# A mixture-of-experts kernel: one more product split by a second Strassen–Winograd level, other places for the W2 mixtures, and another order in the last part

## The chip, the cores and the metric

The kernel runs on one core of a Trainium2 chip. The metric is device time in microseconds (us) for one launch. All arithmetic of the stages told of here is in fp32.

## The reference, cut to what matters

Eight sequences of 1024 tokens with 512 features go through two sublayers. The first is a causal attention whose queries, keys and outputs are built from table sines and cosines; the change does not touch it. The second is a feed-forward with eight experts:

```python
x = x + attention(layernorm(x))
x = x + ffn(layernorm(x))

probs = softmax(x @ Wr + br);  topk_p, topk_e = top_k(probs, 2)
# each of the 8 sequences has 160 places at each expert; later tokens are dropped
buf = zeros((8, 8 * 160, 512)).at[expert, sequence, place].add(x_rep * keep)
h = relu(einsum('enc,ech->enh', buf, W1) + b1)      # 512 -> 2048
y = einsum('enh,ehc->enc', h, W2) + b2              # 2048 -> 512
out[token] = sum over its two experts of y * probability * keep
```

So each of the eight experts multiplies 1280 rows by its W1 (512 x 2048) and its W2 (2048 x 512). This takes about three fifths of the kernel's time.

## The kernel before, in words

**Stages.** Attention runs over 32 pairs of a sequence and a group of four heads (scores at L683, exponentials at L703, values at L717), the router's steps lie beside it. Then come the experts, in 16 *parts*: for each expert one part of three pairs of row blocks (`nh` = 3, even number i) and one of two (`nh` = 2, odd i). A row block is 128 rows; a pair of them makes the upper and the lower half of a matrix product. Part 0 is the first, part 15 the last.

**Both layers by Strassen–Winograd.** Each product of two matrices is cut into 2 x 2 blocks and done with seven products, p1 to p7, of mixtures (sums and differences) of the blocks instead of eight plain ones. `gather(i)` fetches a part's rows by indirect DMA on POOL, transposes them on PE and forms the mixtures of the rows. `mix_w1(i, q)` forms the mixtures of W1 for one of eight column groups q, `mix_w2(e)` those of W2: four subtractions on DVE (L1067 to L1070) for each of eight slices k, one `yield` a slice, so that the caller can place them between other work. `load_w2` brings W2 in by eight DMAs of 512 KB.

**Layer 1.** For each q, a `Hidden` object runs p1 to p7 (L1239) and leaves the seven mixtures of the hidden values in `hid`. The p7 and p4 of one q are issued within the next (`layer1(this, before, final)`). After each product a `Hidden` takes one step of each generator in its `asides`.

**Layer 2, part 0.** `layer2(i, block, hid, aside)` does one pair of blocks with seven products of eight matmuls of 128 x 256 (one per slice k; each fp32 matmul shows as two instructions in the profile), L1340. Three such calls make up part 0's second layer.

**Layer 2, parts 1 to 15.** `layer2_quad` does two pairs of blocks at once. Four of the products are plain (L1473); the pair (part of `hid`, weight) names them: 0·0, 4·3, 5·4 and 6·5. The other three, 1·1, 2·2 and 3·6, are split once more by the same scheme: `SECOND` lists them, `mix` (L1422 to L1429) forms eight mixtures of their operands on DVE, and `second_level` runs seven chains of 128 x 128 matmuls (L1439) into three PSUM banks, with ACT copies (L1450 to L1464) and three DVE additions. `places` finds room for these mixtures: with `nh` = 2 in columns of `hid` that are not in use, with `nh` = 3 in new tiles of the gather's pools. Parts with `nh` = 3 do their third pair of blocks by `layer2` after the quad. Below, "quad" is a call of `layer2_quad`, and "run" is one product by the second level.

**Outputs.** For each pair of blocks, y1 (upper rows) and y2 (lower rows) are built in SBUF in left and right halves (y11, y12, y21, y22). `gate` multiplies by the router's probability (ACT, L1310), `send` adds the rows to `out` by an indirect DMA on POOL (L1315). Two of these may hit the same rows of `out`, so each waits for the one before it. The y tiles come from the pool `yp` with four buffers.

**What sets the order.** PE, ACT, DVE and SP run their instructions in the order in which the program issues them; the program interleaves by hand, with the generators (`next` is one step, `some(n, g)` is n steps, `rest(g)` what is left). PSUM has a pool of six banks for products, `ps_p`. In the loop over the parts, W2's mixtures for an expert are issued one slice per q from q = 2 on, the remaining ones before the second layer; for part 0 two slices are issued after q = 6 and the others after layer 1, right ahead of its second layer. In a part with `nh` = 2 the generator `aside` (the gather of the next part) is issued in steps within the quad, with `nh` = 3 and in part 0 within `layer2`. The core of that loop:

```python
for q in range(NHQ):
    ...
    if i and q > 1:
        next(mixes, None)
    tiles = layer1(Hidden(i, q, parts, hid, [ending]), tiles, q == NHQ - 1)
    ...
    elif i == 0 and q == NHQ - 2:
        mixes = mix_w2(0)
        some(2, mixes)
if i == 0:
    find_rows(1)
rest(mixes)
```

Of the kernel before, what the change touches and what calls it, by code (L numbers as in the profile page):

```python
# [11 lines left out]
F32 = mybir.dt.float32  # L12
# [9 lines left out]
P = 128  # L22
# [51 lines left out]
def preln_attn_moe_kernel(  # L74
# [106 lines left out]
    ident = const.tile([P, P], F32, name="ident")  # L181
# [876 lines left out]
    def mix_w2(e):  # L1058

        w = w2_tiles[e]  # L1060
        t = pools["w2p"].tile([P, NHQ, 3, DC], F32, name="w2_t")
        b11, b12 = w[:, :, 0, :DC], w[:, :, 0, DC:]
        b21, b22 = w[:, :, 1, :DC], w[:, :, 1, DC:]
        t2, t3, t4 = (t[:, :, n, :] for n in range(3))
        w2_tiles[e] = [b11, b21, b22, b12, t2, t3, t4]
        for k in range(NHQ):
            TT(t3[:, k, :], b12[:, k, :], b22[:, k, :], ALU.subtract)  # L1067
            TT(b12[:, k, :], b12[:, k, :], b11[:, k, :], ALU.subtract)  # L1068
            TT(t2[:, k, :], b22[:, k, :], b12[:, k, :], ALU.subtract)
            TT(t4[:, k, :], b21[:, k, :], t2[:, k, :], ALU.subtract)  # L1070
            yield
# [231 lines left out]

    def outputs(i, block):
# [9 lines left out]
        def send(r, y):  # L1314
# [5 lines left out]
            if i == 0:  # L1320
                tc.keep_in_program_order(ins)

# [6 lines left out]
    def layer2(i, block, hid, aside):  # L1329
# [8 lines left out]
        def product(ps, part, weight, first, last):  # L1338
# [5 lines left out]
            next(aside, None)  # L1344

        gate, send = outputs(i, block)
        (y1, y11, y12), (y2, y21, y22) = new_y(), new_y()
        low, high = b2_tiles[e][:, :DC], b2_tiles[e][:, DC:]

        def side_product():  # L1350
            side = bank()
            product(side, 1, 1, True, True)
            TT(y11, y11, side, ALU.add)
# [4 lines left out]
        nc.scalar.copy(y11, top)  # L1358
        if plain_first:
            side_product()  # L1360
        mid = bank()
        product(mid, 4, 3, True, False)
        nc.scalar.copy(y22, mid)
        product(top, 5, 4, False, False)
        nc.scalar.copy(y12, top)
        if not plain_first:
            side_product()
            product(top, 6, 5, False, False)
            TT(y22, y22, top, ALU.add)
        product(mid, 2, 2, False, True)  # L1370
# [3 lines left out]
        send(0, y1)  # L1374
        if plain_first:
            product(top, 6, 5, False, False)
            TT(y22, y22, top, ALU.add)
        TT(y22, y22, high, ALU.add)
# [4 lines left out]
        send(1, y2)  # L1383

# [17 lines left out]
    SECOND = [(1, 1), (2, 2), (3, 6)]  # L1402

    def layer2_quad(i, hid, aside, before_last):

        e = chunks[i][0]
        ws = w2_tiles[e]
        free = places(i, hid)
        low, high = b2_tiles[e][:, :DC], b2_tiles[e][:, DC:]
        two = range(2)  # L1410

        def split(t, part_of):
            return [[part_of(t[:, 4 * k : 4 * k + 4], c) for c in two] for k in two]

        def mix(n):
            part, weight = SECOND[n]
            a = split(hid, lambda t, c: t[:, :, part, c * P : (c + 1) * P])
            b = split(ws[weight], lambda t, c: t[:, :, c * P : (c + 1) * P])
            (a11, a21), (a12, a22) = a
            (b11, b12), (b21, b22) = b  # L1420
            t1, t2, t3, t4, s2, s3, s4 = free[:7]
            TT(t1, b12, b11, ALU.subtract)  # L1422
            TT(s3, a11, a21, ALU.subtract)
            TT(a21, a21, a22, ALU.add)
            TT(t2, b22, t1, ALU.subtract)
            TT(s2, a21, a11, ALU.subtract)
            TT(t3, b22, b12, ALU.subtract)
            TT(s4, a12, s2, ALU.subtract)
            TT(t4, b21, t2, ALU.subtract)  # L1429
            return (  # L1430
                (a11, b11), (a12, b21), (s4, b22), (a22, t4), (a21, t1), (s2, t2), (s3, t3)
            )
# [4 lines left out]
        def chain(ps, pair, first):  # L1437
            for k in range(4):
                nc.tensor.matmul(  # L1439
                    ps, lhsT=pair[0][:, k, :], rhs=pair[1][:, k, :], start=first and k == 0,  # L1440
                    stop=k == 3, skip_group_check=True,
                )

        def second_level(n, pairs):
            m1, m2, m3, m4, m5, m6, m7 = pairs
            c = free[7 + n]
            c11, c12, c21, c22 = (c[:, k, :] for k in range(4))
            u, v, z = (bank()[:, :P] for _ in range(3))
            chain(u, m1, True)
            nc.scalar.copy(c11, u)  # L1450
            next(aside, None) if n < 2 else None
            chain(v, m5, True)
            nc.scalar.copy(c21, v)
            chain(u, m6, False)
            nc.scalar.copy(c12, u)
            chain(z, m2, True)
            TT(c11, c11, z, ALU.add)
            chain(u, m7, False)
            nc.scalar.copy(c22, u)
            chain(v, m3, False)  # L1460
            TT(c22, c22, c21, ALU.add)
            TT(c12, c12, v, ALU.add)
            chain(u, m4, False)
            nc.scalar.copy(c21, u)  # L1464
            return [c[:, 2 * b : 2 * b + 2, :] for b in two]

# [3 lines left out]
        def product(ps, part, weight, first, last):  # L1470
            for b in two:
                for k in range(NHQ):
# [6 lines left out]

        gate, send = zip(*(outputs(i, b) for b in two))  # L1480
        some(2, aside)
        pairs = mix(0)
        top, mid = bank(), bank()
# [366 lines left out]
```

## Time and profile before

| | us |
|---|---|
| median of three runs | 3196.95 (3196.12 to 3196.96) |
| the profiled execution | 3195.52 |
| its span, which the profile's times refer to | 3193.8 |
| TensorE clock granted, mean | 0.997 |

By stage, from the windows view of the trace (times from the span's start):

| stage | from – to | length | PE busy | DVE busy |
|---|---|---|---|---|
| attention, router, first gather | 0 – 1258 | 1258.0 | 1206.9 | 1004.1 |
| layer 1 of part 0, with the last router steps | 1258 – 1342 | 84.0 | 81.6 | 55.7 |
| second layer of part 0 | 1342 – 1422 | 80.0 | 77.0 | 28.4 |
| layer 1 of part 1 (two pairs of blocks) | 1422 – 1470 | 48.0 | 48.0 | 29.1 |
| quad of part 1 | 1470 – 1516.3 | 46.3 | 46.3 | 36.5 |
| layer 1 of part 2 (three pairs of blocks) | 1516.3 – 1588.5 | 72.2 | 72.2 | 46.3 |
| quad and third pair of part 2 | 1588.5 – 1659.1 | 70.6 | 70.6 | 40.1 |
| quad of part 15 | 3132.8 – 3179.3 | 46.5 | 46.4 | 25.8 |
| tail after the last matmul | 3179.3 – 3193.8 | 14.5 | 0 | 0.4 |

Parts 3 to 14 repeat parts 1 and 2. A busy PE is one that has a matmul under way; the ends of matmuls are modelled, so the distance between starts is the better measure of what one costs. Idle time in front of an instruction is given in brackets with what ended it. The profile's line numbers are those of the kernel before.

### The profile page before, as it was taken

The page shows a single profiled execution, that of the slowest core. Times are in us where ns is not written, and L with a number is a line of the kernel's source. Part 1 is how long each engine was busy: PE and PEld are TensorE (multiplying, and loading weights), DVE is VectorE, ACT ScalarE, POOL GpSimd, SP SyncE. Part 2 cuts the span into 40 slices and gives each one's busy share as a digit, 9 for nine tenths or more (in the row PEclk, how much of TensorE's full clock was granted, in tenths as well). Part 3 has the DMA queues.
Part 4 walks back from the last instruction along what each step waited for, and adds up shares of the span by engine and source line. Part 5 has one row for each costly group of instructions (what it writes and reads, how often), then busy time and mean ns, then how long its engine had stood idle before and what let it go on. Part 6 is the DMA issues. An engine that isn't in the chain of part 4 may idle for free.

```text
span 3193.8 us, 51293 instructions
## 1 busy us (share of the span) xinstructions
PE 3122.6 (98%) x19726; PEld 2145.4 (67%) x19726; DVE 2209.3 (69%) x4643; ACT 1664.9 (52%) x2554; POOL 426.8 (13%) x387
## 2 busy tenths in 40 slices
PE   5999999999999999999999999999999999999998
PEld 2444444444444444689698698698698698698687
DVE  8888878888788775637657657656657656656654
ACT  7888888888888885413423423323323323323322
POOL 3000202020111123411011011011011011011010
PEclk9999999999999999999999999999999999999999
DMA  5435454554645353423423433434433334334331
GB/s 166 147 100 165 120 159 132 148 140 138 184 108 159 80 166 88 141 60 98 147 57 98 140 62 103 130 63 112 120 70 110 115 74 114 107 80 116 96 60 21
DMA packets 288547, 358.72 MB, mean 112 GB/s; under 512 B 28376, under 2 KB 199088, under 8 KB 276272
## 3 DMA queue, kind: packets, MB, share of 16 engines
q1 hardware_dynamic: 264944, 312.20, 33.3%
q0 software_dynamic: 22912, 43.22, 7.4%
q8 instruction: 157, 2.57, 0.4%
q14 instruction: 86, 0.70, 0.1%
q10 hardware_dynamic: 448, 0.02, 0.0%
HBM read 207.02 MB, written 81.22 MB: 90 GB/s over the span
## 4 chain that ended last, share of the span: by engine, by line
PE 79%; DVE 3%; ACT 1%; issue 1%; DMA 0%; SPq 0%; POOLq 0%; DVEq 0%; ACTq 0%
PE ps_p L1239 30%; PE ps_p L1473 13%; PE av L717 9%; PE ps_p L1439 9%; PE ps_s L683 9%; PE ps_p L1340 7%; ACT e L703 1%; PE ps_s L215 1%; PE ps_s L697 1%; DVE qk_f L524 1%; DVE qk_r L447 0%; DVE xT L837 0%; DMA qk<-qk_r 0%; DVE v L447 0%; SPq L608 0%
## 5 line engine op out<-in xcount | busy, mean ns | idle before, releaser
L703 ACT ACTIVATE e<-ps_s 128x1024 f32<-128x1024 f32 (+1 forms) x640 | 569.6, 937 | 183.3 <-PE ps_s L683 110.2
L683 PE MATMUL ps_s<-qk 64*128 64x512 f32 (+3 forms) x3072 | 597.3, 505 | 28.6 <-DMA qk<-qk_r 12.4
L717 PE MATMUL av<-e,v 128*64 128x512 f32 (+3 forms) x3072 | 523.4, 490 | 0.0
L683 PEld LDWEIGHTS ps_s<-qk 64*128 64x128 f32 x3072 | 262.3, 187 | 216.1 <-issue 106.4
L717 PEld LDWEIGHTS av<-e,v 128*64 128x64 f32 x3072 | 200.5, 137 | 283.1 <-issue 267.1
L1239 PE MATMUL ps_p<-xe,w 128*128 128x256 f32 (+1 forms) x1024 | 317.6, 433 | 1.1 <-issue 1.1
L1239 PE MATMUL ps_p<-xe_s,t 128*128 128x256 f32 (+1 forms) x1024 | 317.7, 433 | 0.0
L1239 PE MATMUL ps_p<-xe,t 128*128 128x256 f32 (+1 forms) x1024 | 317.7, 433 | 0.0
L1315 POOL DMA_INDIRECT out_dram<-y,slots x80 | 127.1, 1589 | 1234.0 <-ACT y L1310 1016.6
L768 POOL DMA_INDIRECT slot_d<-token,slot x128 | 159.2, 1244 | 988.5 <-issue 612.3
L1282 DVE TENSOR_TENSOR hid<-hid 128x256 f32<-128x256 f32 (+1 forms) x128 | 64.0, 500 | 283.0 <-ACT hid L1280 283.0
L1239 PEld LDWEIGHTS ps_p<-xe_s,t 128*128 128x128 f32 x1024 | 193.8, 190 | 82.0 <-ACT hid L1249 2.5
L1239 PEld LDWEIGHTS ps_p<-xe,t 128*128 128x128 f32 x1024 | 194.2, 190 | 80.4 <-issue 0.4
L1239 PEld LDWEIGHTS ps_p<-xe,w 128*128 128x128 f32 x1024 | 193.7, 190 | 79.4 <-issue 1.2
L1473 PE MATMUL ps_p<-w_t,hid 128*128 128x256 f32 x960 | 212.2, 379 | 0.0
L1473 PE MATMUL ps_p<-w,hid 128*128 128x256 f32 x960 | 209.6, 379 | 0.0
L1473 PEld LDWEIGHTS ps_p<-w,hid 128*128 128x128 f32 x960 | 182.4, 190 | 26.3
L1473 PEld LDWEIGHTS ps_p<-w_t,hid 128*128 128x128 f32 x960 | 180.1, 190 | 23.2
L1239 PE MATMUL ps_p<-xe_s,w 128*128 128x256 f32 (+1 forms) x512 | 158.9, 433 | 0.6 <-ACT p L1255 0.6
L1249 ACT COPY hid<-ps_p 128x256 f32<-128x256 f32 (+1 forms) x128 | 54.2, 423 | 179.6 <-PE ps_p L1239 170.9
L1340 PE MATMUL ps_p<-w,hid 128*128 128x256 f32 x640 | 144.8, 381 | 2.5 <-DVE w L1068 2.5
L697 PEld LDWEIGHTS <-keys_b 64*128 64x128 bf16 x1536 | 80.8, 95 | 89.5 <-issue 71.5
(300 smaller groups left out, 4959.6 us busy)
## 6 DMA issues: line engine op xcount, KB each, us to landing
w<-in_L_ffn_W_dram SPq DMA_DIRECT2D x256, 256.0 KB, 3.4
w<-in_L_ffn_W_dram SPq DMA_DIRECT2D x64, 512.0 KB, 7.4
qk<-qk_c SPq DMA_DIRECT2D x124, 256.0 KB, 4.5
qk<-qk_r SPq DMA_DIRECT2D x120, 256.0 KB, 4.5
qk_base<-base_d SPq DMA_DIRECT2D x28, 1024.0 KB, 7.5
xn_d<-xn SPq DMA_DIRECT2D x72, 256.0 KB, 2.4
rows_d<-xg SPq DMA_DIRECT2D x70, 256.0 KB, 2.1
x_mid<-in_L_attn_x_dram SPq DMA_DIRECT2D x16, 1024.0 KB, 8.9
```

The costliest lines, as they stand in the source:

```text
L683: nc.tensor.matmul(ps[:, a, at : at + w], lhsT=pair[r, 1, kb * P : (kb + 1) * P], rhs=pair[r, 0, q0 : q0 + w], start=at == 0, stop=not own ...
L697: nc.tensor.matmul(out_, lhsT=keys_b[r, part, :], rhs=late, start=False, stop=part == 1, skip_group_check=True,)
L703: nc.scalar.activation(e, ps[:, :, :n], AF.Exp, scale=UNIT * UNIT / math.sqrt(2 * DH))
L717: nc.tensor.matmul(av[a * 64 : (a + 1) * 64, q0 - 512 * h :], lhsT=vt[:, kb, 2 * pr + a, :], rhs=es[i][:, a, at : at + w], start=kb == 0, ...
L768: queued = nc.gpsimd.indirect_dma_start(out=slot_d[b], out_offset=bass.IndirectOffsetOnAxis(ap=idx, axis=0), in_=src, in_offset=None,)
L1239: nc.tensor.matmul(ps, lhsT=weights[:, k, :], rhs=rows[:, k, :], start=first and k == 0, stop=last and k == 1, skip_group_check=True,)
L1249: nc.scalar.copy(self.blocks[0], self.top)
L1282: TT(g1, g3, h22, ALU.add)
L1315: ins = nc.gpsimd.indirect_dma_start(out=out, out_offset=bass.IndirectOffsetOnAxis(ap=meta[:, e, jj[r], 0:1], axis=0), in_=y, in_offset=No ...
L1340: nc.tensor.matmul(ps, lhsT=hid[:, k, part, cols], rhs=ws[weight][:, k, :], start=first and k == 0, stop=last and k == NHQ - 1, skip_group ...
L1439: nc.tensor.matmul(ps, lhsT=pair[0][:, k, :], rhs=pair[1][:, k, :], start=first and k == 0, stop=k == 3, skip_group_check=True,)
L1473: nc.tensor.matmul(ps[:, b * DC : (b + 1) * DC], lhsT=hid[:, k, part, b * P : (b + 1) * P], rhs=ws[weight][:, k, :], start=first and k == ...
```

## The change

**A fourth product by the second level.** In all 15 quads p5 (product 4·3) becomes a run too. A class `Second` replaces `SECOND`, `mix` and `second_level`: `weights()` and `left()` are generators of four DVE operations each for the two sides, `both()` issues them interleaved, `run()` issues the chains. In parts with `nh` = 2 the weights of p5 and p2 are mixed within layer 1 (two operations at each of q = 3 to 6), their left sides in the quad; in parts with `nh` = 3 both sides are mixed in the quad. The order of a quad becomes: plain 0·0, run of p5, plain 5·4, run of p2, plain 6·5, run of p3, [with `nh` = 3: two products of the third pair of blocks], run of p4. `layer2` is now a generator that yields after each product, so that the third pair can be issued in pieces.

**W2's mixtures in smaller portions.** `mix_w2` yields after each subtraction. In part 0 the mixtures are created after q = 4 and one operation is handed out per product in q = 6, two per product in q = 7; the rest follows layer 1, ahead of `find_rows(1)` (before, behind it). In the other parts four operations are issued at q = 2 and 3 and eight from q = 4 on.

**The last part.** Its order becomes: runs of p2, p3 and p4, then the plain product 6·5 by blocks, with y21 and y22 built beforehand. y1 is gated and sent within the run of p4. The four scatters of the last part wait for the last one of part 14 and are declared free of each other.

**Pools.** `ident` gets its place from another pool, and `yp` has five buffers instead of four.

The diff, cut:

```diff
@@ mix_w2
-            TT(t3[:, k, :], b12[:, k, :], b22[:, k, :], ALU.subtract)
-            ...
-            yield
+            for to, x1, x2 in ((t3, b12, b22), (b12, b12, b11), (t2, b22, b12), (t4, b21, t2)):
+                TT(to[:, k, :], x1[:, k, :], x2[:, k, :], ALU.subtract)
+                yield
@@ outputs: send
+            if i + 1 == len(chunks):
+                tc.add_manual_dep(ins.ins, sent[i - 1][-1].name, ...)
+                for other in sent.get(i, ()):
+                    tc.declare_no_dep(ins.ins, other, reason="rows of their own")
+            sent.setdefault(i, []).append(ins.ins)
@@
+    class Second:
+        OPERANDS = {2: (1, 1), 3: (2, 2), 4: (3, 6), 5: (4, 3)}
...
+        def weights(self):
+            ...
+            for to, x1, x2 in ((t3, b22, b12), (t1, b12, b11), (t2, b22, t1), (t4, b21, t2)):
+                TT(to, x1, x2, ALU.subtract)
+                yield
+        def left(self):
+            ...
+            for to, x1, x2, op in (
+                (s3, a11, a21, ALU.subtract), (a21, a21, a22, ALU.add),
+                (s2, a21, a11, ALU.subtract), (s4, a12, s2, ALU.subtract),
+            ):
+                TT(to, x1, x2, op)
+                yield
+        def both(self):
+            w, a = self.weights(), self.left()
+            for gen, count in ((w, 2), (a, 2), (w, 1), (a, 1), (w, 1), (a, 1)):
+                some(count, gen)
+            ...
+        def run(self, c, between=lambda: None, late=lambda: None):
+            ...
+            chain(u, a11, b11, True)
+            nc.scalar.copy(c11, u)
+            between()
+            chain(v, a21, t1, True)
+            nc.scalar.copy(c21, v)
+            chain(u, s2, t2, False)
+            nc.scalar.copy(c12, u)
+            chain(z, a12, b21, True)
+            TT(c11, c11, z, ALU.add)
+            chain(u, s3, t3, False)
+            nc.scalar.copy(c22, u)
+            late()
+            chain(v, s4, b22, False)
+            TT(c22, c22, c21, ALU.add)
+            TT(c12, c12, v, ALU.add)
+            chain(u, a22, t4, False)
+            nc.scalar.copy(c21, u)
@@ layer2_quad
+        last_part = nh == 2
+        ask(2)
+        if last_part:
+            rest(second[5].left())
+        else:
+            second[5].both()
         product(top, 0, 0, True, False)
         for b in two:
             nc.scalar.copy(y11[b], of(top, b))
-        product(mid, 4, 3, True, True)
-        some(3, aside)
-        c = second_level(0, pairs)
-        ...
+        if last_part:
+            rest(second[2].left())
+        ask(2)
+        five = second[5].run(c5)
+        second[3 if last_part else 2].both()
+        ask()
         product(top, 5, 4, False, False)
         for b in two:
             nc.scalar.copy(y12[b], of(top, b))
-            TT(y12[b], y12[b], of(mid, b), ALU.add)
+        add_to(y12, five)
+        add_to(y11, second[2].run(c, ask))
+        second[4 if last_part else 3].both()
+        ask()
+        if i + 1 == len(chunks):
+            add_to(y12, second[3].run(c))
+            ...
+            four = second[4].run(c, late=first_rows)
+            for b in two:
+                TT(as_pair(y21[b]), as_pair(low), four[b], ALU.add)
+                TT(as_pair(y22[b]), as_pair(high), five[b], ALU.add)
+            for b in two:
+                product(top, 6, 5, False, True, [b])
+                for y in (y22[b], y21[b]):
+                    TT(y, y, of(top, b), ALU.add)
+                    gate[b](1, y)
+                send[b](1, y2[b])
+            return extra
         product(top, 6, 5, False, True)
+        for b in two:
+            TT(as_pair(y22[b]), as_pair(of(top, b)), five[b], ALU.add)
...
+        add_to(y12, second[3].run(c, ask))
...
+        if not last_part:
+            first_rows()
+            second[4].both()
+            some(2, extra)
+        before_last()
...
+        add_to(y21, second[4].run(c5, right_halves, first_rows if last_part else lambda: None))
@@ the loop over the parts
+            if nh == 2:
+                second = seconds(i, hid)
+                early_sums = itertools.chain(second[0][5].weights(), second[0][2].weights())
...
-                    next(mixes, None)
+                    some(4 if q < 4 else 8, mixes)
+                if 2 < q < 7:
+                    some(2, early_sums)
+                beside = [ending] if i or q < NHQ - 2 else [mixes] * (q + 3 - NHQ)
-                tiles = layer1(Hidden(i, q, parts, hid, [ending]), tiles, q == NHQ - 1)
+                tiles = layer1(Hidden(i, q, parts, hid, beside), tiles, q == NHQ - 1)
                 if i == 0 and q == NHQ // 2:
...
-                elif i == 0 and q == NHQ - 2:
                     mixes = mix_w2(0)
-                    some(2, mixes)
+            rest(mixes)
             if i == 0:
                 find_rows(1)
-            rest(mixes)
```

## The prediction

> **What bounds the kernel now.** I read the page first: parts 1 and 2 (who is busy, and when), then the chain that ended last, and then the timeline of the stages that the diff touches.
>
> ```profile
> span 3193.8 us, 51293 instructions
> PE 3122.6 (98%) x19726; PEld 2145.4 (67%) x19726; DVE 2209.3 (69%) x4643; ACT 1664.9 (52%) x2554; POOL 426.8 (13%) x387
> ...
> PE ps_p L1239 30%; PE ps_p L1473 13%; PE av L717 9%; PE ps_p L1439 9%; PE ps_s L683 9%; PE ps_p L1340 7%; ACT e L703 1%; PE ps_s L215 1%; PE ps_s L697 1%; DVE qk_f L524 1%; DVE qk_r L447 0%; DVE xT L837 0%; DMA qk<-qk_r 0%; DVE v L447 0%; SPq L608 0%
> ```
>
> PE is busy for the whole span, and in the expert stages the chain hardly leaves it. There a microsecond of PE work is a microsecond of time, as long as DVE and ACT keep their work beside it. A busy share does not give the price of one matmul, though, so the timeline of PE is next, in the second layer of part 2:
>
> ```profile
> 1602.39 1.05 PE L1439 MATMUL ps_p<-w,hid 128*128 128x128 f32 x8
> 1603.28 1.06 PE L1439 MATMUL ps_p<-xe,hid 128*128 128x128 f32 x8
> ...
> 1608.64 7.07 PE L1473 MATMUL ps_p<-w_t,hid 128*128 128x256 f32 x32
> 1615.55 1.05 PE L1439 MATMUL ps_p<-w,hid 128*128 128x128 f32 x8
> ```
>
> Starts count here, not durations, which overlap. A plain product over two blocks (32 instructions, since each fp32 matmul is two) takes 1615.55 - 1608.64 = 6.91 us, or 215.9 ns each. A second-level product (7 chains of 8) takes 1608.64 - 1602.39 = 6.25 us, 0.893 us a chain, 111.6 ns each. No row between carries an idle time.
>
> Two places are not bound by PE's own work. In part 0's second layer PE waits for the W2 mixtures on DVE, and then runs slowly (columns of the second view: PE, PEld, DVE, ACT and POOL busy, PEclk, DMA share, GB/s):
>
> ```profile
> 1353.87 1.20 PE L1340 MATMUL ps_p<-w,hid 128*128 128x256 f32 x2 [1.01 <-DVE w L1068]
> 1355.59 1.22 PE L1340 MATMUL ps_p<-w,hid 128*128 128x256 f32 x2 [0.51 <-DVE w L1068]
> 1356.60 5.68 PE L1340 MATMUL ps_p<-w_t,hid 128*128 128x256 f32 x16
> ```
> ```profile
> 1357.00:1359.00 2.00, 2.00 (x6) 1.61 (x5) 0.00 (x0) 0.22 (x1) 0.00 (x0) 0.50 0.58 185
> ```
>
> At the very end PE has finished (3179.26 by the chain), and the last two scatters stand in a row:
>
> ```profile
> 3179.28 0.27 ACT L1464 COPY hid<-ps_p 128x128 f32<-128x128 f32 x1 [1.52 <-PE ps_p L1439]
> ```
> ```profile
> 3180.62 1.55 POOL L1315 DMA_INDIRECT out_dram<-y,slots  x1 [5.01 <-ACT y L1310]
> 3186.14 1.56 POOL L1315 DMA_INDIRECT out_dram<-y,slots  x1 [3.97 <-DMA out_dram<-y,slots]
> ```
>
> **What the skill says.** TensorE: Matmul & The Clock Gate, "Wait — 56ns, not 53.3ns?": warm matmuls start N / 2.4 GHz plus about 2.5 ns apart. The trace fits if an fp32 pass takes two cycles a column: 512 / 2.4 + 2.5 = 215.8 against 215.9 ns; 256 / 2.4 + 2.5 = 109.2 against 111.6 ns. The fixed part is why a split product saves less than one eighth. The same page, "What's actually happening": the clock is halved after about 3.4 us of idleness and comes back after about as much work. The trace agrees on 0.50, but here waits of at most 1.01 us each, close together, were enough. PSUM — Partial Sum Buffer, "PSUM bank collisions raise a hardware error": access has to be guarded by bank, not by address; the trace before has no such wait in the quad. DMA: Bandwidth & Descriptors, "Two DMAs through the same engine are not ordered": only a completion semaphore orders them; the 3.97 us above are such an order.
>
> **The change, part by part.** The first 1316 us have the same instructions in the same order on every engine (ident only changes its pool), so they stay.
>
> *p5 by the second level*, in all 15 quads (parts 1 to 15): one 6.91 us product out, one 6.25 us run in. -0.656 x 15 = **-9.8 us**, if nothing waits. DVE gets 8 mixing operations of 0.605 us (pitch) and 3 additions of 0.29 us, 5.7 us more a quad (its 16 y operations only change operands); ACT gets five copies of 0.27 us and loses two of 0.37. What hides them:
> - Three-block parts (7): p5's mixtures used to have p1 and p5 in front of them, 13.8 us; now p1 alone, 6.91. At 1588.57 the products began and the layer-1 tail left DVE at 1592.7, 4.1 us in. Then come t3, t1, s3, a21: a21 is done at about +6.6, and chain 2 wants it at 6.91 + 0.89 = +7.8. t2 and s2 come at 7.8 for +8.7, s4 at 9.0 for +11.4. Margin 0.9 to 1.2 us. It holds because W2's mixtures are no longer at this place: rows 1592.59 to 1596.02 of DVE held 3.4 us of them. They go to q 4 to 6 of layer 1, as four more operations (1.8 us) a round, where DVE idled 1.9 to 3.6 us before L1282. Almost full, not over.
> - Two-block parts (8): weight mixtures of p5 and p2 (two per round, 1.3 us) go into q 3 to 6, where the 64 rounds idle 127.6 / 64 = 2.0 us before L1282. The left sides need 4 operations, done at about +5.5 against +7.8.
> - Later runs: 8 mixtures end 5.6 us after the run before, and a 6.91 us step lies between (in three-block parts two products of the third block take that place before the last run).
> - The gather's transposes and sums (six and four) crowd DVE around p3's run: behind until about 17.6 us after p2's run, while layer 1 wants t1 at 20.7. ACT's first copy there is about 0.8 us early.
> - SP's order is unchanged. W2's next load may start later, when p3's run has read W2, but 6.25 us ahead of the quad's end; b2's load, in front of it, went out only 3.5 us ahead (1512.83, next part at 1516.3). POOL's order is the same too; y1's scatters wait longer, and the fifth y buffer covers that.
>
> *W2 mixtures of part 0 per product.* The stage should take 21 products of 3.453 us = 72.5 us and takes 1421.60 - 1341.82 = 79.8; lost 7.25 us. 0.65 of it is the wait for y at L1377, whose order stays. Now 21 of the 32 operations lie within layer 1 (8 before), in DVE's idle 3.9, 1.9 and 1.5 us there; 11 remain. By DVE's pitches of 0.34 to 0.46 us the last b12 is ready at about 1351.5, and PE wants it at 1348.73 + 7 x 0.432 = 1351.75. W2 is there: the eight loads land 1322 to 1333. The index row for part 1's gather now stands behind these 11, so its four gathers on POOL start 6.5 us later; its rows are due 50 us on. **-6.4 us** (-3 if PE waits once more and the clock falls; -6.6 at best).
>
> *Last part.* The final product comes by blocks, block 1 in block 0's bank. In the built program its first matmul waits for DVE's second read of that bank: two additions at 0.335 us pitch and a hop, about +0.95 us on PE. No row before shows it: 0 to 1.3. After PE's end two additions, two gates of 0.5 us and POOL: the last scatter starts at about +1.5, where it was 3186.14 - 3179.26 = +6.9. Block 0's has left 4 us earlier, and the y1 scatters earlier still. From there to the end 7.66 us as before. -5.4 + 0.95 = **-4.4 us** (-3 to -5.4).
>
> Sum: -9.8 - 6.4 - 4.4 = -20.6 us. The profiled execution took 3195.52 (span 3193.8 and 1.7 around it), so 3174.9; the median shown is 1.4 above that execution: **3176.3 us**.
>
> **The rivals.** Main case, 0.80: 3174 to 3179.
> *Only p5 pays*, 0.08: PE still waits in part 0, or the bank wait and slow gates eat the end: -9.8 and about 2 more, 3185. For it: both places hang on margins under 0.5 us. Against: two thirds of the mixtures do move.
> *Quads wait a little*, 0.07: 0.4 us each, from halved cover, x 15 = 6 us: 3182. For it: margins near 1 us, and a fuller DVE. Against: each is positive, from rows measured in the same stage.
> *Slower*, 0.05: a late a21 or t2 stops PE at chain 2 or 3 of the new run, in all quads; waits close together halve the clock, as in part 0, where 2.5 us of shown waits cost some 6.6. The point is 20.6 / 15 = 1.4 us a quad. DVE would have to be 2.5 us later than I place it, for instance if rounds with eight W2 operations no longer fit and leave it behind; then 2 us a quad with its clock make about 5: 15 x 5 - 20.6 = +54, 3251. Against: 1.8 us fits the idle time, and q 7 has no mixture any more.
> That the chains do not shorten PE can be left out: three such runs a quad are in the trace.
>
> **How the numbers follow.** 0.2% is 6.4 us, about what a measurement can tell. Main case, "only p5" and most of "waits a little" lie beyond it: faster 0.92, same 0.04, slower 0.04. The range takes in the main case, its low end with no bank wait and a full gain in part 0 (3176.3 - 3, about 3173), and "waits a little": 3173 to 3183.
>
> **What would show it.** Right: two-block quads of 45.75 us and three-block second layers of 69.9 without idle time on PE; the second layer of part 0 near 73 us with PEclk 1.00; one wait of about 0.95 us for DVE's y addition in the last product; last scatters without a DMA wait, 9 us of tail after PE. Wrong: idle time before second-level chains with DVE as releaser, PEclk below 1.00 in a quad, or ACT copies that wait for DVE ahead of layer 1.

## The result, and the profile after

The changed kernel takes 3177.55 us in the median of four runs (3177.08 to 3178.59), the kernel before 3196.95 (3196.12 to 3197.28): 19.4 us less, a ratio of 0.9940 (95% interval 0.9923 to 0.9957). The forecast was 3176.3, with a range of 3173 to 3183. The profiled execution took 3177.95 us, span 3176.2; it lies 17.6 us below the one before, where the sum of the prediction said 20.6. The head of the page after:

```profile
span 3176.2 us, 52225 instructions
PE 3112.0 (98%) x20086; PEld 2147.5 (68%) x20086; DVE 2303.7 (73%) x4808; ACT 1680.4 (53%) x2599; POOL 424.1 (13%) x387
```

More matmul instructions, more DVE work, and still a shorter span: PE is as full as before (98%), and the added instructions are shorter ones. Where the time went is read from the starts of stages on PE, which the timeline gives (the end of PE is the last start plus the 0.893 or 3.455 us that this chain or product takes by the distance between starts):

| stage | before | after | difference | forecast |
|---|---|---|---|---|
| up to part 0's second layer | 1341.82 | 1342.36 | +0.54 | 0 |
| second layer of part 0 | 79.78 | 73.30 | -6.48 | -6.4 |
| layer 1, two / three pairs of blocks | 48.35 / 72.24 | 48.35 / 72.24 | 0 | 0 |
| quads of parts 1, 3 ... 13 (7) | 46.38 | 46.06 | 7 x -0.32 | 7 x -0.66 |
| second layers of parts 2, 4 ... 14 (7) | 70.56 | 69.90 | 7 x -0.66 | 7 x -0.66 |
| last quad, to PE's end | 46.38 | 46.74 | +0.36 | +0.29 |
| tail behind it | 14.73 | 9.60 | -5.13 | -5.4 |

The forecast of +0.29 for the last quad is p5's -0.66 and the bank wait's +0.95. The 0.54 us of the first row arose ahead of part 0's layer 1 (which starts at 1259.20 before and 1259.74 after), in code that did not change; that layer 1 itself takes 82.62 us in both.

The timeline of PE in part 0's second layer, after:

```profile
1342.36 10.52 PE L1352 MATMUL ps_p<-w,hid 128*128 128x256 f32 x48
1352.72 3.62 PE L1352 MATMUL ps_p<-w_t,hid 128*128 128x256 f32 x16
...
1363.76 3.72 PE L1352 MATMUL ps_p<-w_t,hid 128*128 128x256 f32 x16 [0.51 <-DVE y L1395]
```

Where before had three waits for DVE's mixtures and a halved clock, 48 instructions (three products) now go in one row and take 10.36 us. The wait for the y addition is still there, as forecast. DVE wrote the last mixture that the third product needs here:

```profile
1351.15 0.43 DVE L1069 TENSOR_TENSOR w<-w 128x256 f32<-128x256 f32 x1
```

Done at 1351.58; PE wants it at 1342.36 + 2 x 3.455 + 7 x 0.432 = 1352.29. The margin was 0.7 us, forecast as 0.25.

The second layer of part 2, PE:

```profile
1582.31 7.07 PE L1537 MATMUL ps_p<-w,hid 128*128 128x256 f32 x32
1589.22 1.05 PE L1474 MATMUL ps_p<-w,hid 128*128 128x128 f32 x8
1590.11 1.06 PE L1474 MATMUL ps_p<-xe,hid 128*128 128x128 f32 x8
1591.00 1.06 PE L1474 MATMUL ps_p<-xe 128*128 128x128 f32 x8
```

and DVE beside it, with the mixture that the second chain needs:

```profile
1588.25 0.69 DVE L1454 TENSOR_TENSOR hid<-hid 128x512 f32<-128x512 f32 x1
```

a21 is done at 1588.94, 6.6 us after the products begin, and the second chain starts at 7.8 without a wait: the prediction's figures.

The end, POOL's timeline of after:

```profile
3158.26 1.55 POOL L1316 DMA_INDIRECT out_dram<-y,slots  x1 [80.74 <-ACT y L1311]
3160.12 1.56 POOL L1316 DMA_INDIRECT out_dram<-y,slots  x1 [0.31 <-issue]
3163.98 1.55 POOL L1316 DMA_INDIRECT out_dram<-y,slots  x1 [2.30 <-ACT y L1311]
3168.54 1.56 POOL L1316 DMA_INDIRECT out_dram<-y,slots  x1 [3.01 <-ACT y L1311]
```

No scatter waits for a DMA any more; the last starts 1.94 us after PE's end at 3166.60, where before it was 7.07. On PE the one new wait is in the last product, whose block 1 goes into the bank that DVE still reads for block 0:

```profile
3163.15 3.72 PE L1537 MATMUL ps_p<-w_t,hid 128*128 128x256 f32 x16 [0.84 <-DVE y L1590]
```

What the forecast did not have is in two-block quads. The timelines of PEld (PE's weight loads), ACT and DVE in the quad of part 1, after, at the step from p3's run to p4's:

```profile
1505.50 0.97 PEld L1474 LDWEIGHTS ps_p<-hid 128*128 128x128 f32 x8 [0.25 <-ACT hid L1483]
```
```profile
1505.01 0.27 ACT L1498 COPY hid<-ps_p 128x128 f32<-128x128 f32 x1 [2.84 <-DVE hid L1495]
1505.17 0.27 ACT L1483 COPY hid<-ps_p 128x128 f32<-128x128 f32 x1
```
```profile
1503.56 0.96 DVE L1187 TENSOR_TENSOR xe_s<-xe,xe_s 128x768 f32<-128x768 f32 x1
1504.44 0.28 DVE L1490 TENSOR_TENSOR hid<-hid,ps_p 128x128 f32<-128x128 f32 x1
1504.64 0.28 DVE L1495 TENSOR_TENSOR hid<-hid 128x128 f32<-128x128 f32 x1
```

Read from below: the gather's sums hold up DVE's addition L1495; it reads c21, which ACT's L1498 overwrites, so ACT waits 2.84 us; behind that copy on ACT stands the first copy of p4's run, and the third chain of that run may not write its bank before this copy. By the starts on PE, the third chain begins 0.22 us late, and the chain after it another 0.1.

### The profile page after: what moved, and what is told of

The parts are those of the page before. It is cut to its first block, busy times and chain, and to the rows that moved or that the text cites. A ratio compares the mean times of both kernels' runs of the same rounds, so it can differ in the third digit from the quotient of the medians.

```text
span 3176.2 us, 52225 instructions
## 1 busy us (share of the span) xinstructions
PE 3112.0 (98%) x20086; PEld 2147.5 (68%) x20086; DVE 2303.7 (73%) x4808; ACT 1680.4 (53%) x2599; POOL 424.1 (13%) x387
## 4 chain that ended last, share of the span: by engine, by line
PE 78%; DVE 4%; ACT 1%; issue 1%; DMA 0%; SPq 0%; POOLq 0%; POOL 0%; DVEq 0%; ACTq 0%
PE ps_p L1238 30%; PE ps_p L1474 10%; PE ps_p L1537 10%; PE av L718 10%; PE ps_s L684 9%; PE ps_p L1352 8%; ACT e L704 1%; PE ps_s L216 1%; PE ps_s L698 1%; DVE qk_f L525 1%; DVE qk_r L448 0%; DMA qk<-qk_r 0%; DVE xT L838 0%; DVE xe L1174 0%; DVE xe_s L1186 0%
## 5 line engine op out<-in xcount | busy, mean ns | idle before, releaser
L1352 PE MATMUL ps_p<-w,hid 128*128 128x256 f32 x640 | 142.9, 379 | 0.0
L1474 PE MATMUL ps_p<-w,hid 128*128 128x128 f32 x1104 | 141.8, 275 | 0.0
L1311 ACT ACTIVATE y<-y,slots 128x256 f32<-128x256 f32 (+1 forms) x120 | 65.9, 578 | 142.8 <-DVE y L1389 105.5
L1474 PEld LDWEIGHTS ps_p<-w,hid 128*128 128x128 f32 x1104 | 135.8, 192 | 2.3
```

The lines of the kernel that those rows point to most:

```text
L1311: nc.scalar.activation(part, part, AF.Identity, scale=meta[:, e, jj[r], 1:2].bitcast(F32))
L1352: nc.tensor.matmul(ps, lhsT=hid[:, k, part, cols], rhs=ws[weight][:, k, :], start=first and k == 0, stop=last and k == NHQ - 1, skip_group ...
L1474: nc.tensor.matmul(ps, lhsT=left[:, k, :], rhs=right[:, k, :], start=first and k == 0, stop=k == 3, skip_group_check=True,)
```

## The experiments

The experiments ran in three groups of four. Each group ran on one chip, together with the kernel before; the groups were on different chips. Medians are compared with the kernel before of the same group. The time up to part 0's second layer varies (1340.6 to 1357.7 us in the profiles), while the stages after it agree to some hundredths of a microsecond from chip to chip. So the stage lengths decide; the medians agree with their sums to 3.4 us or better. Two-block quads are those of parts 1 to 13.

### Part 0's mixtures where they were

```diff
-                beside = [ending] if i or q < NHQ - 2 else [mixes] * (q + 3 - NHQ)
+                beside = [ending]
...
-                    mixes = mix_w2(0)
-            rest(mixes)
+                elif i == 0 and q == NHQ - 2:
+                    mixes = mix_w2(0)
+                    some(8, mixes)
             if i == 0:
                 find_rows(1)
+            rest(mixes)
```

> The changed kernel with part 0's W2 mixtures issued as before (two slices after q = 6, the other 24 operations behind the index row and layer 1). If the mixtures' place is worth what the second layer of part 0 shows (79.78 us before, 73.30 us after), that stage returns to 79.8 us, with idle time of PE before L1352 that DVE ends and a granted clock below 1.00 after it, and the median rises by 6.5 us over the changed kernel's 3177.55, to 3184. The rival, that part of the stage's gain belongs to the new order in layer2 (new y tile created later, products yielded one by one), puts the stage at 75 to 78 us and the median at 3179 to 3182.

Measured: 3196.34 us, 0.9961 of before (0.9947 to 0.9974). Second layer of part 0: 78.94 us, the stages behind it as in the changed kernel. PE's waits in that stage:

```profile
PE ps_p L1352 <- DVE w L1069: 3.0, 3, 1.0
PE ps_p L1352 <- DVE y L1395: 0.5, 1, 0.5
```

Three waits of about 1 us return, and a granted clock of 0.50 behind them. So the place of the mixtures is worth 5.64 of the 6.48 us. The other 0.84 fit the length of the clock's dip: by slices of 2 us, PEclk was 0.73, 0.50, 0.50, 0.56 before, and 0.92, 0.50, 0.73 in this experiment. At full clock that is 3.4 us missing before and 1.7 here, while PE's waits for these mixtures are 0.5 us longer here (3.0 against 2.5). That is a reading of two traces and not a test of its own; the new order inside `layer2` may have a share.

### p5 as a plain product

```diff
-        five = second[5].run(c5)
+        mid = bank()
+        product(mid, 4, 3, True, True)
+        y2, y21, y22 = zip(*(new_y() for _ in two))
+        for b in two:
+            nc.scalar.copy(y22[b], of(mid, b))
...
-        add_to(y12, five)
+        for b in two:
+            TT(y12[b], y12[b], y22[b], ALU.add)
```

Its mixtures are left out, y22 is built by additions to the copy.

> The changed kernel with p5 as a plain product over two blocks in all 15 quads; the order, the other three runs and the rest are as changed. My account from the two traces: a three-block second layer gains 0.66 us by the run, a two-block quad only 0.33 in parts 1 to 13 (0.33 is lost again to a late ACT copy), the last quad 0.66. Then two-block quads go from 46.06 to 46.39 us, three-block second layers from 69.90 to 70.56, and the median from 3177.55 to about 3185.2 (7 x 0.33 + 8 x 0.66 = 7.6). The rival, that the 0.33 us come from the new order or from the gather and not from p5's run, leaves the loss in: two-block quads of 46.7 us, and 3187.4 (15 x 0.656 = 9.8).

Measured: 3201.98 us, 0.9983 (0.9974 to 0.9991). Three-block second layers 70.56 us, two-block quads 46.71. My account was wrong and its rival right: p5's run is worth 0.66 us in every quad, 15 x 0.655 = 9.8, as forecast; the 0.33 us are lost with p5 plain too. They belong to the new order, in which p4's run follows p3's directly. The trace of the kernel before supports this, for the same wait stands there. ACT in the quad of part 1, before (L1464 is the last copy of p3's run, L1461 the addition that it waits for, L1450 the first copy of p4's run), and ACT's waits in parts 1 to 14:

```profile
1503.76 0.27 ACT L1464 COPY hid<-ps_p 128x128 f32<-128x128 f32 x1 [1.91 <-DVE hid L1461]
...
1511.17 0.27 ACT L1450 COPY hid<-ps_p 128x128 f32<-128x128 f32 x1 [4.53 <-PE ps_p L1439]
```
```profile
ACT hid L1464 <- DVE hid L1461: 13.4, 7, 1.9
```

Product 6·5 stood between the two runs and kept PE busy for 6.9 us, so nothing came of the late copy. The change took this cover away, and the wait that then reached PE could be read before the change.

### The last part: order of products and order of scatters

The scatters in order, as before: the manual dependency and the two lines of `declare_no_dep` are left out. The old order of products:

```diff
         if i + 1 == len(chunks):
             add_to(y12, second[3].run(c))
             for b in two:
                 TT(y1[b], y1[b], b2_tiles[e], ALU.add)
-            ...
-            four = second[4].run(c, late=first_rows)
-            ...
+            first_rows()
+            product(top, 6, 5, False, True)
+            ...
+            add_to(y21, second[4].run(c5))
```

Both undone:

> The changed kernel with the last part in the old order: y1 sent after p3's run, product 6.5 over both blocks, then the run of p4, and every scatter waits for the one before. Expected from the traces: PE's part of the last quad falls from 46.74 to 45.73 us (0.84 us of wait for L1590's addition and what follows it are gone), the tail from PE's end rises from 9.6 to 14.7 us, together +4.1 us: 3181.7. The rival, that only the freed scatters matter and the order of products does not, gives the same total here and is told apart by the run with the new order and ordered scatters.

Measured: 3197.27 us, 0.9966 (0.9952 to 0.9979); PE's quad 45.73, tail 14.7, together 60.4 us.

Only the scatters in order:

> The changed kernel whose last part keeps its new order of products, while each of the four last scatters waits for the one before, as in the kernel before. Before, scatters in order started 5.5 us apart. From y1's first at PE's end minus 8.3 us the last would start at about PE's end + 8.2 instead of + 1.9: a tail of about 15.9 us instead of 9.6, PE's last quad as in the changed kernel (46.74 us): 6.3 us more than the changed kernel. Rival: the new order by itself already spreads the scatters enough, so that the tail is 11 us or less.

Measured: 3199.39 us, 0.9970 (0.9958 to 0.9982). POOL's timeline:

```profile
3184.57 1.55 POOL L1316 DMA_INDIRECT out_dram<-y,slots  x1 [4.09 <-DMA out_dram<-y,slots]
3190.23 1.56 POOL L1316 DMA_INDIRECT out_dram<-y,slots  x1 [4.10 <-DMA out_dram<-y,slots]
```

PE ends at 3181.81, the last scatter starts 8.4 us later, tail 16.0.

Only the old order of products:

> The last part with the old order of products (y1 sent, product 6.5 over both blocks, run of p4 last) and the four scatters free of each other. PE's quad falls to 45.73 us. After PE's end stand two y additions, four gates at 0.4 us on ACT and two scatters on POOL, 1.9 us apart: the last starts at about PE's end + 4, a tail of some 11.5 us, together 57.2 us against 56.3 of the changed kernel. Then nearly all of the 4.1 us of this part come from the freed scatters and 0.9 from the product by blocks. Rival: the gates and POOL's issue stand in a row longer, tail 13 or more, and the order is worth 2 us and up.

Measured: 3193.49 us, 0.9950 (0.9935 to 0.9966); last scatter 3.4 us after PE's end, tail 11.45. The four together, PE's last quad and tail in us:

| | scatters in order | scatters free |
|---|---|---|
| y1 early, run of p4 last | 45.73 + 14.7 = 60.4 | 45.73 + 11.45 = 57.2 |
| product 6·5 by blocks last | 46.74 + 16.0 = 62.7 | 46.74 + 9.6 = 56.3 |

The freed scatters bring 3.2 us by themselves and the new order 0.9 on top of them. The new order alone would have cost 2.3: 1.0 is PE's wait for the bank, and 1.3 is a longer tail, because y1's scatters leave later and the other two queue behind them.

### The gather's sums moved

```diff
-        add_to(y12, second[3].run(c, ask))
+        add_to(y12, second[3].run(c))
         for b in two:
             TT(y1[b], y1[b], b2_tiles[e], ALU.add)
+        ask()
```

> One line moved: in two-block quads the last step of the next part's gather (a transpose and the four sums of 0.96 us, L1184 to L1187) is issued after the additions of p3's run and of y1, not inside that run. Theory: those sums hold up DVE's c22 addition (L1495), ACT's copy L1498 waits for that, ACT's copy L1483 of p4's run stands behind it, and the third chain of p4's run waits for its bank. Then the idle time of PEld before L1474 with ACT L1483 as releaser (1.7 us in 7 waits) disappears, two-block quads of parts 1 to 13 fall from 46.06 to 45.73 us, and the median falls by 2.3 us to 3175.2. Rivals: the sums now hold up the additions of p4's run and with them ACT ahead of layer 1, so that the loss only moves (no change, 3177.5), or the 0.33 us are not from this wait at all (46.06 stays).

Measured: 3208.01 us, 1.0002 of before (0.9993 to 1.0010); all of the change's gain is gone. Quads do fall to 45.73 us. But layer 1 of the next part takes 74.5 us in five parts and 76.2 in two, where it took 72.24. PE's waits after part 0:

```profile
PE ps_p L1238 <- ACT hid L1248: 13.5, 7, 1.9
```

ACT and DVE at the end of part 1's quad, in two timelines:

```profile
1525.61 0.27 ACT L1498 COPY hid<-ps_p 128x128 f32<-128x128 f32 x1 [2.91 <-PE ps_p L1238]
1526.21 0.91 ACT L1311 ACTIVATE y<-y,slots 128x256 f32<-128x256 f32 x2 [0.34 <-DVE y L1532]
1527.03 0.46 ACT L1248 COPY hid<-ps_p 128x384 f32<-128x384 f32 x1
```
```profile
1525.24 0.28 DVE L1495 TENSOR_TENSOR hid<-hid 128x128 f32<-128x128 f32 x1
```

A wait of the same kind now stands at p4's run: PE is named as its releaser, but L1498 starts 0.09 us after DVE's L1495 ends, and the matmul named writes another bank. Behind p4's run there is no slack: p6 of layer 1 needs the copy L1248, which stands behind L1498 and the gates (L1311) on ACT. Which of the two makes it late is tested below. The first rival was right in kind, but it expected no change in total, and the loss is far larger.

### The middle value at a place of its own

```diff
             chain(v, a21, t1, True)
-            nc.scalar.copy(c21, v)
+            held = a21[:, 0, :]
+            nc.scalar.copy(held, v)
...
-            TT(c22, c22, c21, ALU.add)
+            TT(c22, c22, held, ALU.add)
```

> In every run the middle value that ACT copies from the second chain goes to a place of its own (the dead columns of a21) and not to c21; so ACT's last copy of a run, into c21, need not wait until DVE has read the middle value (L1495). Theory: that wait on ACT is what delays the first copy of p4's run and with it the third chain. Two-block quads of parts 1 to 13 fall from 46.06 to 45.73 us although DVE keeps its order, layer 1 stays at 72.24, three-block second layers at 69.90; 7 x 0.33 = 2.3 us less than the changed kernel in total. Rival: DVE's late additions themselves hold PE through the banks that they read; then 46.06 stays.

Measured: 3174.57 us, 0.9940 (0.9927 to 0.9954), 20.6 us less than before beside it. Two-block quads 45.73, layer 1 72.24. DVE and ACT, in two timelines:

```profile
1503.78 0.28 DVE L1496 TENSOR_TENSOR hid<-hid 128x128 f32<-128x128 f32 x1
```
```profile
1502.89 0.27 ACT L1499 COPY hid<-ps_p 128x128 f32<-128x128 f32 x1 [1.58 <-PE ps_p L1474]
1503.73 0.27 ACT L1483 COPY hid<-ps_p 128x128 f32<-128x128 f32 x1 [0.57 <-PE ps_p L1474]
```

DVE's addition is as late as it was (L1496 is the former L1495), but ACT's copy goes ahead of it and waits for PE alone. The cause of the 0.33 us is shown: the copy's wait for the late addition, through the shared place c21.

With the sums moved as well:

> The gather's sums moved behind the additions of p3's run, as in the run before this one, and the middle value at a place of its own. With the sums moved alone, quads took 45.73 us but the layer 1 behind them 74.5 to 76.2 instead of 72.24. If ACT's wait for DVE's addition was the cause there too, both are gone: quads of 45.73, layer 1 of 72.24, total as with the middle value apart alone. If DVE was simply too late for layer 1 (the sums themselves, or the y additions in front of ACT's gates), layer 1 stays above 72.24, by 0.5 us or more.

Measured: 3194.31 us, 0.9998 (0.9990 to 1.0007); quads 45.73, layer 1 74.6 to 76.3. The rival held. ACT there:

```profile
1511.49 0.91 ACT L1311 ACTIVATE y<-y,slots 128x256 f32<-128x256 f32 x2 [3.02 <-DVE y L1533]
1512.30 0.46 ACT L1248 COPY hid<-ps_p 128x384 f32<-128x384 f32 x1
```

ACT's gates wait for the y additions, which DVE makes behind sums and W1 mixtures, and layer 1's first copy stands behind the gates. Taking away one of two things that L1248 waits for moved nothing: the sums are better where the change has them.

### Two banks in the last part

```diff
         top = bank()
+        tops = [top, bank()] if i + 1 == len(chunks) else [top, top]
...
-        of = lambda ps, b: ps[:, b * DC : (b + 1) * DC]
+        of = lambda ps, b: tops[b][:, b * DC : (b + 1) * DC]
...
-                        ps[:, b * DC : (b + 1) * DC],
+                        tops[b][:, b * DC : (b + 1) * DC],
```

> In the last part only, the two blocks of the plain products have a PSUM bank each. Theory: the 0.84 us of PE's wait for L1590 exist because DVE reads block 0 in the bank that block 1 is written to; then PE runs through, the last quad takes 45.73 instead of 46.74 us on PE, and the tail from PE's end stays at 9.6 us: 1.0 us less in total. Rival: block 1's additions and gates now stand behind block 0's on DVE and ACT, so that the tail grows to 10.2 or more and less than half is gained.

Measured: 3176.56 us, 0.9946 (0.9931 to 0.9961). PE's waits hold L1590 no more, the last quad takes 45.73 us on PE and the tail 9.23: 1.0 us less on PE, as expected, and 0.4 less behind it. Together they are 55.0 us, against 57.2 with the old order and free scatters: without the bank wait the new order is worth 2.2 us and not 0.9.

### W2's mixtures in the other parts paced as before

```diff
-                    some(4 if q < 4 else 8, mixes)
+                    some(4, mixes)
```

> The changed kernel with W2's mixtures of later experts issued as before, four operations a q and the last eight ahead of the quad. It tests the margins of the prediction: in three-block parts p5's mixtures then stand behind 8 operations, 3.4 us on DVE, a21 is done at about +10.0 us where the second chain wants it at +7.8. Expected 2.2 to 3 us of idle time on PE in p5's run with DVE L1454 or L1443 as releaser, three-block second layers of 72.1 to 73 us instead of 69.90, 15 to 22 us in total, more if the granted clock falls; two-block quads stay at 46.06. Rival: the layer-1 tail on DVE ends so much earlier with fewer mixtures in q = 4 to 6 that the cover holds; then 69.90 stays and the new pace is not needed.

Measured: 3200.78 us, 1.0021 of before (1.0013 to 1.0030), slower. Three-block second layers 72.7 us in four parts and 74.0 to 74.3 in three. PE in part 2, and the windows view at the same place (columns: PE, PEld, DVE, ACT and POOL busy, PEclk, DMA share, GB/s):

```profile
1593.57 1.79 PE L1474 MATMUL ps_p<-xe,hid 128*128 128x128 f32 x8 [2.16 <-DVE hid L1454]
1595.16 1.91 PE L1474 MATMUL ps_p<-xe 128*128 128x128 f32 x8
```
```profile
1594.00:1596.00 2.00, 2.00 (x11) 2.00 (x10) 1.92 (x4) 0.27 (x1) 0.00 (x0) 0.50 0.00 0
```

This is the prediction's rival "slower", brought about in the three-block parts: a21 is late by 2.2 us. The clock fell only behind three of the seven waits, those of the three longer stages; behind the other four it stayed at 1.00. Seven waits of 2.16 us are 15.1 us, the stages together lose 24.1. Without the new pace of these mixtures p5's run would have lost more than the whole change brings.

### Four y buffers

```diff
-                    for name, bufs in (("w2p", 1), ("yp", 5), ("bp", 1)):
+                    for name, bufs in (("w2p", 1), ("yp", 4), ("bp", 1)):
```

> Four y buffers instead of five. The prediction said that the fifth covers the later scatters of y1. In three-block parts the third pair's y1 then waits until the scatter of the quad's first y1 has landed, about 4.4 us later than ACT's copy L1364 goes now; behind that copy on ACT stands the first copy of p4's run, with 4.0 us of slack. Expected: ACT waits about 4 us at L1364, PE loses 0 to 1 us in a three-block second layer (69.90 to 70.9), 0 to 7 us in total. Rival: nothing waits at all, 69.90, and the buffer is not needed; or the wait reaches PE through more than one copy and its clock falls, 72 us and more.

Measured: 3190.59 us, 0.9943 (0.9928 to 0.9958), three-block second layers 69.90. ACT's wait in part 2 (the other six three-block parts have one too, 32.3 us for all seven):

```profile
ACT y L1364 <- DMA out_dram<-y,slots: 4.6, 1, 4.6
```

The wait exists, with the expected length, and none of it reaches PE. So the prediction's sentence that the fifth buffer covers y1's later scatters is not what decides: ACT's slack does.

### A version with the repairs together

It takes the middle value apart and the two banks, moves product 6·5 ahead of 2·2 in part 0's first block, and gates the last y2 before the last product:

```diff
-                for y in (y22[b], y21[b]):
-                    TT(y, y, of(top, b), ALU.add)
-                    gate[b](1, y)
+                for y in (y22[b], y21[b]):
+                    nc.vector.scalar_tensor_tensor(y, of(top, b), p, y, ALU.mult, ALU.add)
```

> The changed kernel with the middle value of each run at a place of its own; two PSUM banks in the last part; in the first block of part 0 product 6.5 ahead of 2.2, so that DVE's reading of its bank (the 0.51 us of wait for L1395) is hidden; and the last y2 gated before its last product, which DVE then adds with the gate's factor in one operation each (no gate on ACT after PE's end). Expected against the changed kernel: two-block quads 45.73 (7 x 0.33 = 2.3 us), part 0's second layer 72.6 instead of 73.30 (0.7), last quad 45.73 instead of 46.74 on PE (1.0), tail 8.6 instead of 9.6 (the two gates of 0.5 us that stand in a row, less what is left of it by 0.1): 4.8 us in total, some 0.15%. Rivals: the earlier 6.5 meets W2 mixtures that are not ready and PE waits in part 0 (stage above 73.3); DVE's combined operation takes as long as addition and gate together (tail stays at 9.2).

Measured: 3187.49 us, 0.9933 (0.9919 to 0.9946), 20.9 us less than before beside it. Quads 45.73 throughout, the last one too; part 0's second layer 73.25, tail 9.55. Two of the four repairs brought next to nothing, the ones in part 0 and in the tail. In part 0 the wait for DVE only made room for another:

```profile
1368.98 3.72 PE L1352 MATMUL ps_p<-w_t,hid 128*128 128x256 f32 x16 [0.46 <-issue]
```

In the program, the first matmul of product 6·5 waits for ACT's copy of its bank (L1377), which 2·2 had covered. In the tail the combined operation is short (0.44 us), but POOL's scatter came 0.77 us after it, where behind ACT's gate it had come 0.27 us after. Beside the two banks alone nothing is gained: there the last scatter starts 1.84 us after PE's end, here 1.91:

```profile
3175.72 0.87 DVE L1590 SCALAR_TENSOR_TENSOR y<-ps_p,slots,y 128x256 f32<-128x256 f32 x2 [2.57 <-PE ps_p L1534]
```
```profile
3177.36 1.56 POOL L1316 DMA_INDIRECT out_dram<-y,slots  x1 [1.89 <-DVE y L1590]
```

By stages this version is some 3.4 us below the changed kernel (7 x 0.33, 1.01 on PE at the end, 0.1 of the rest). It did not run beside it; the version with four y buffers, which has the changed kernel's stages, took 3.1 us more in the same group.

## Why the prediction was right, and where not

**p5 by the second level.** Right in mechanism and size: 0.655 us a quad, 9.8 in all, shown by making it plain. Only the reason given for the size is incomplete: a chain's matmul takes 111.6 ns, half of a 256-column one 108.0, and 56 times these 3.6 ns are the 0.2 us by which a run is longer than seven eighths of a plain product. The fixed 2.5 ns that the prediction cites would give 0.07 of it (an estimate); the rest is not explained here. The cover in three-block parts was read rightly to 0.1 us, and the experiment with the old pace shows that the margin was needed. Wrong was one step of the paragraph, "DVE around p3's run: behind until about 17.6 us after p2's run": it asked only when layer 1 wants its mixtures. It did not ask which of ACT's copies waits for the additions behind that work, though it listed such copies as a sign, and though the trace before has this wait seven times. That cost 7 x 0.33 = 2.3 us, through a buffer that is written twice (c21), and through p4's run standing directly behind p3's. So the rival "quads wait a little" came partly true: 0.33 us in seven quads and not 0.4 in fifteen, and not from the halved cover that it named.

**W2 mixtures of part 0.** -6.48 against -6.4. 5.64 are shown by the mixtures' place; the rest is only argued. The deadline on DVE came out 0.45 us easier than worked out.

**Last part.** -5.13 in the tail and +1.01 on PE, -4.1 in sum, against -5.4, +0.95 and -4.4. The bank wait was there (0.84 us, and 0.17 until PE was in step again), and two banks take it away. Mis-sized is the last scatter's start, +1.94 us and not +1.5; a part of this is the end of PE from which one counts, for from the modelled end that the prediction used (3179.26 before, 3166.87 after) it is +1.67. What the prediction did not separate: most of it comes from the freed scatters, and the new order of products without them is a loss of 2.3 us.

**The sum.** -17.6 in the profiled executions, against -20.6: 2.3 from the two-block quads, 0.3 from the last part, 0.5 from the unchanged stages ahead of it. The medians, -19.4, lie nearer to the sum than the two executions that were profiled. This nearness is luck of 1 to 2 us in the stages ahead, and it shows nothing of how good the working was.

## What to carry to other kernels

When work is added to an engine that is not the bound, look not only for who waits for the new results, but for every instruction that shares a buffer with what is queued behind them: here a copy on a third engine had to wait until a late addition had read its old value, and in-order queues passed that on to PE. Such a wait can be in the trace before, harmless as long as another piece of work covers it; when a change moves that piece, ask what covers the wait then. Giving the value a place of its own took the wait away and lengthened no stage; moving the work made another copy on ACT late, at a higher price. And try the parts of a change in pairs: freeing the scatters brought 3.2 us by itself, reordering the products cost 2.3 by itself, and together they brought 4.1.

## What the runs showed of the hardware that was not expected

The same idle time on PE did not always bring the granted clock down. With the old pace of W2's mixtures PE waits about 2.16 us in seven stages; the clock fell to 0.50 behind three of these waits and stayed at 1.00 behind four. With the gather's sums moved it waits about 1.93 us seven times; the clock fell behind two and stayed at 1.00 behind five. An idle time of 0.84 us (the changed kernel, last product) left it at 1.00. So idle times well below the 3.4 us that the prediction cites can be enough, and need not be. What decides was not tried.

This makes two prices for one wait. Where the clock stayed, the stages lost 2.8 us for 2.16 and 2.3 for 1.93; where it fell, 4.1 to 4.4 and 4.0. Each fall was equally long: summed over windows of half a microsecond, 1.71 us of full clock were missing in each of these five, which is 3.4 us at 0.50. In part 0's second layer it was 1.71 us with the mixtures where they were, and twice as much, 3.42, in the kernel before.

The stages from part 0's second layer on repeated to about 0.03 us over all fourteen traces, wherever an experiment's edit did not touch them. The same code ahead of them took between 1340.6 and 1357.7 us. About half of this has one place. In the eight traces of two of the three groups, layer 1 of part 0 takes 91.2 to 92.7 us, in the other six 82.62. In each of the eight, ACT stands idle for 7.9 to 10.6 us ahead of one copy (L1248), the view names no engine of this core as the releaser ("remote"), and PE waits 6.6 to 7.0 us for that copy. Why was not tried and stays open.
